# Key transposes in 32x32 blocks on VectorE in place of 128x128 transposes on TensorE, with pooling, softmax and sorted key rows in that layout

## The chip, the cores and the metric

The kernel runs on one core of a Trainium2 chip. The metric is the time of one execution on the device, in microseconds (us). Each run was made on one chip together with runs of the kernel before, so a ratio always compares runs of the same chip. The runs of this study fell on at least four chips, which the results call chips 2, 3, 11 and 13; the number will matter. Every kernel in this document gave correct results, those with useless extra work too.

## The reference, cut to what matters

There are B = 1024 sequences of up to 100 steps with 128 features. A GRU runs over all 100 steps; its hidden states are the keys. A small network scores each key against an item, a masked softmax over the steps gives weights, and the weighted sum of the keys is pooled. The first 100 pooled features, transposed, are the attention weights of a second recurrent loop, the AUGRU, which runs over the same keys. Each sequence takes its AUGRU state at its own last step into a final network.

```python
_, gru_seq = lax.scan(gru_step, h0, swapaxes(item_historical_embedding, 0, 1))
keys = swapaxes(gru_seq, 0, 1)                       # B x 100 x 128
score = _mlp(concat([keys, q, keys - q, q * keys]), att_layers, relu)
attn = softmax(where(mask == 1, score, -inf), axis=1)
pooled = einsum('bt,btd->bd', attn, keys)
att_seq = pooled.T[:T]
def augru_step(h, (x_t, a_t)):
    r = sigmoid(concat([h, x_t]) @ Wr.T + br)
    u = a_t * sigmoid(concat([h, x_t]) @ Wu.T + bu)
    h_hat = tanh(concat([h * r, x_t]) @ Wh.T + bh)
    return (1 - u) * h + u * h_hat
aug_out = scan(augru_step, h0, (keys, att_seq))
attention_feature = aug_out[b, sequential_length[b] - 1]
# ... final three-layer network on user, item, history and attention_feature
```

## The kernel before

Features lie on the 128 partitions and sequences on the columns, in two halves of 512 columns whose steps alternate. In the GRU each half-step's new state is transposed on TensorE, so that pooling can weight a sequence by a scalar of its partition, and so that a sequence's keys can be written to memory as one row. Four steps make a row of 2 KB.

```python
def transpose(self, t):
    q, n = divmod(t, G)                               # G = 4
    ...
    p = pa.tile([P, GH, P], F32, tag="a", name="pk")
    for g in range(GH):                               # 4 groups of 128 sequences
        nc.tensor.transpose(p[:, g, :], h[:, ts(g, P)], ident)
    nc.scalar.copy(kt[:, :, n, :], p)
    if n == G - 1:
        nc.sync.dma_start(out=keys_d[q]..., in_=kt...)
```

The AUGRU runs on sequences sorted by length, longest first, so that the width of a step (the columns still alive) falls from 512 to about 20. The keys come back from memory in sorted order through indirect gathers on GpSimd, 128 rows each, up to four per half and group of four steps. TensorE transposes them again and ScalarE copies them.

```python
def load_rows(q, i, widths):
    ...
    for g in range(-(-widths[q * G] // P)):           # up to 4 gathers
        gather(r[:, g, :], keys_d[q], g, i)           # 128 rows x 2 KB
def load_key(t, i):
    ...
    for g in range(-(-w // P)):
        nc.tensor.transpose(p[:, ts(g, P)], r[:, g, ts(n, P)], ident)
    k = wp.tile([P, HB], F32, name="k3", bufs=6)
    nc.scalar.copy(k[:, :w], p[:, :w])
def step(t, i):                                       # one half-step of the AUGRU, shortened
    pr = gate(wr, h); nc.scalar.activation(pr, pr, Sigmoid); nc.vector.tensor_mul(r, h, pr)
    pu = gate(wu, h); nc.scalar.activation(pu, pu, Sigmoid); nc.vector.tensor_mul(u, pu, at)
    ph = gate(wh, r); nc.scalar.activation(ph, ph, Tanh)
    # VectorE: ph -= h; ph *= u; h += ph
```

The attention weights are sorted between the loops with 32 matmuls against 0/1 matrices that GpSimd builds.

Of the kernel before, what the change touches and what calls it, by code (L numbers as in the profile page):

```python
# [11 lines left out]
I32 = mybir.dt.int32  # L12
AF = mybir.ActivationFunctionType
# [5 lines left out]
P = 128  # L19
# [5 lines left out]
GH = HB // P  # L25
A0, A1 = 80, 40
# [16 lines left out]
NQ = T // G  # L43

AHEAD = 2

# [8 lines left out]
def kernel(ctx: ExitStack, tc: tile.TileContext, a: dict, out: bass.AP):  # L55
# [15 lines left out]

    nc = tc.nc
# [3 lines left out]
    keys_d = [dram.tile([B, G * P], F32, name=f"keys_d{q}") for q in range(NQ)]  # L76
    mask_d = dram.tile([T, B], BF16, name="mask_d")
    inv_d = dram.tile([B, 1], I32, name="inv_d")
    over_d = dram.tile([1, 1], I32, name="over_d")
    att_d = [dram.tile([T, HB], F32, name=f"att_d{i}") for i in range(NH)]  # L80
    rlen_d = dram.tile([NG, P], F32, name="rlen_d")
# [11 lines left out]
    pooled = const.tile([P, NG, P], F32, name="pooled")  # L93
    alive = const.tile([P, NG, T], F32, name="alive")
    idx = const.tile([P, GH, NH], I32, name="idx")
# [4 lines left out]
    def gather(dst, src, g, i):  # L100

        nc.gpsimd.indirect_dma_start(  # L102
            out=dst,
            out_offset=None,
            in_=src,
            in_offset=bass.IndirectOffsetOnAxis(ap=idx[:, g, i : i + 1], axis=0),
        )
# [3 lines left out]
    def load_rows(q, i, widths):  # L111

        r = mid.tile([P, GH, G * P], F32, tag="once", name="rows") if q == 0 else (
            rows["pool"].tile([P, GH, G * P], F32, name="rows")
        )
        for g in range(-(-widths[q * G] // P)):
            gather(r[:, g, :], keys_d[q], g, i)
        rows[q, i] = r

    def gru_phase(pools):  # L120
# [41 lines left out]
        nc.gpsimd.memset(hist, 0.0)  # L162
        q0 = pre.tile([P, B], F32, name="q0")
# [15 lines left out]
        def load_later():  # L179
# [8 lines left out]
            mask_i = mid.tile([P, NG, T], I32, name="mask_i", tag="once")  # L188
            nc.sync.dma_start(
                out=mask_i, in_=a["mask"].rearrange("(g p) t -> p g t", p=P)  # L190
            )
            on = pre.tile([P, NG, T], F32, name="on")
            nc.vector.tensor_scalar(on, mask_i, 1.0, None, ALU.is_equal)
            later["on"] = on
            yield
# [8 lines left out]
            nc.vector.tensor_copy(step, step_i)  # L204
            nc.vector.tensor_tensor(
# [59 lines left out]
            ids = pre.tile([P, NG], I32, name="ids")  # L265
            nc.gpsimd.iota(ids, pattern=[[P, NG]], base=0, channel_multiplier=1)
            own = pre.tile([P, NG], F32, name="own")
            nc.vector.tensor_copy(own, ids)
# [14 lines left out]
            for g in range(NG):  # L283
                nc.gpsimd.indirect_dma_start(
                    out=inv_d,
                    out_offset=bass.IndirectOffsetOnAxis(ap=rank_i[:, g : g + 1], axis=0),
                    in_=ids[:, g : g + 1],
                    in_offset=None,
                )
                yield  # L290

            ranks = pre.tile([P, HB], F32, name="ranks")
            nc.gpsimd.iota(
                ranks,
                pattern=[[NH, HB]],
                base=0,
                channel_multiplier=0,
                allow_small_or_imprecise_dtypes=True,
            )
            later["ranks"] = ranks  # L300
            for i in range(NH):
                r = pre.tile([P, NG], F32, name=f"rank{i}")
                nc.vector.tensor_scalar_add(r, rank, float(-i))
                later[f"rank{i}"] = r
            nc.sync.dma_start(
                out=idx, in_=inv_d.rearrange("(g p i) o -> p g (i o)", p=P, i=NH)
            )
            yield
            for n, shape in (
# [6 lines left out]
                ("user", [P, B]),  # L316
# [10 lines left out]
        class Half:  # L327
            def __init__(self, i):
                self.i = i
                self.cols = ts(i, HB)  # L330
                self.groups = slice(i * GH, (i + 1) * GH)
# [3 lines left out]
                self.s_b = self.top = self.den = None  # L335
# [4 lines left out]
                self.kt = {}  # L340

# [70 lines left out]
            def transpose(self, t):  # L412

                q, n = divmod(t, G)
                h = self.h.pop(t) if t < T - 1 else self.h[t]
                if n == 0:
                    self.kt[q] = kp.tile([P, GH, G, P], F32, name="kt")
                kt = self.kt[q]
                p = pa.tile([P, GH, P], F32, tag="a", name="pk")
                for g in range(GH):  # L420
                    nc.tensor.transpose(p[:, g, :], h[:, ts(g, P)], ident)  # L421
                nc.scalar.copy(kt[:, :, n, :], p)  # L422
                if n == G - 1:
                    nc.sync.dma_start(
                        out=keys_d[q][self.cols, :].rearrange("(g p) f -> p g f", p=P),
                        in_=kt.rearrange("p g n f -> p g (n f)"),
                    )
# [21 lines left out]
            def score(self, t):  # L449
# [5 lines left out]
                if s == b0:  # L455
                    self.s_b = sp.tile([2 * G, HB], F32, name="s_b", bufs=4)
                nc.sync.dma_start(
                    out=self.s_b[s - b0 : s - b0 + 1, :],
                    in_=self.mv[SC[self.i] : SC[self.i] + 1, :],
# [5 lines left out]
            def softmax(self):  # L465
# [5 lines left out]
                on = later["on"][:, self.groups, b0:b1]  # L471
                s_b, top_old, den_old = self.s_b, self.top, self.den
                e = sp.tile([P, GH, 2 * G + 1], F32, name="e", bufs=6)
                top = sp.tile([P, GH], F32, name="top", bufs=5)
                den = sp.tile([P, GH], F32, name="den", bufs=5)
# [3 lines left out]
                def scores():  # L479
                    pt = pa.tile([P, GH, 2 * G], F32, tag="a", name="pt")  # L480
                    for g in range(GH):
                        nc.tensor.transpose(
                            pt[:, g, :n], s_b[:n, ts(g, P)], ident[:n, :n]
                        )
# [4 lines left out]
                    if j:  # L489
# [5 lines left out]
                        top.unsqueeze(2).to_broadcast([P, GH, n]),  # L495
# [3 lines left out]
                def sums():  # L499
                    nc.vector.tensor_mul(e[:, :, :n], e[:, :, :n], on)  # L500
                    nc.vector.tensor_reduce(den, e[:, :, :n], AX.X, ALU.add)
                    if j:
                        old = sp.tile([P, GH], F32, name="old")
# [15 lines left out]
            def pool(self, count, eng):  # L519
                while count and self.todo:  # L520
                    e, n, t = self.todo.pop(0)
                    if t is None:
                        eng.tensor_mul(  # L523
                            pooled[:, self.groups, :],
                            pooled[:, self.groups, :],
                            e[:, :, n].unsqueeze(2).to_broadcast([P, GH, P]),
# [3 lines left out]
                    acc = pooled[:, self.groups, :]  # L530
                    k = self.kt[t // G][:, :, t % G, :]
                    w = e[:, :, n].unsqueeze(2).to_broadcast([P, GH, P])
                    if t == 0:
                        eng.tensor_mul(acc, k, w)
                    else:
                        d = wp.tile([P, GH, P], F32, name="kw")
# [5 lines left out]
            def weights(self):  # L542


                att = hp.tile([P, GH, P], F32, tag="h", name="att")
                nc.vector.memset(att[:, :, T:], 0.0)
                nc.vector.tensor_mul(
                    att[:, :, :T], pooled[:, self.groups, :T], alive[:, self.groups, :]
                )
                nc.vector.tensor_mul(  # L550
                    att[:, :, :T],
                    att[:, :, :T],
                    self.den.unsqueeze(2).to_broadcast([P, GH, T]),
                )
                self.att = att


            def features(self):
# [8 lines left out]
                nc.gpsimd.tensor_mul(cross, item[:, cols], hist[:, cols])  # L567
                part = kp.tile([P, GH, M0], F32, tag="kt", name="part")
                for g in range(GH):
                    b = slice(self.i * HB + g * P, self.i * HB + (g + 1) * P)  # L570
                    comb = (later["user"][:, b], item[:, b], hist[:, b], cross[:, ts(g, P)])
# [14 lines left out]
        def sort_weights():  # L586


            sums = [ps.tile([P, HB], F32, tag="g", name="pw") for _ in range(NH)]
            for g in range(NG):  # L590
                half = halves[g // GH]
                for i, p in enumerate(sums):
                    here = xp.tile([P, HB], F32, tag="x", name="here")
                    nc.gpsimd.tensor_scalar(
                        here,
                        later["ranks"],
                        later[f"rank{i}"][:, g : g + 1],
                        None,
                        ALU.is_equal,
                    )  # L600
                    nc.tensor.matmul(
                        p,
                        lhsT=half.att[:, g % GH, :],
                        rhs=here,
                        start=(g == 0),
                        stop=(g == NG - 1),
                    )
            for i, p in enumerate(sums):
                att = hp.tile([P, HB], F32, tag="h", name="att_t")
                nc.vector.tensor_copy(att, p)  # L610
                first = ps.tile([P, HB], F32, tag="g", name="first")
                nc.tensor.matmul(
                    first,
                    lhsT=ident[:, 0:1].to_broadcast([P, P]),
                    rhs=att,
                    start=True,
                    stop=True,
                )
                nc.scalar.copy(h3[i], first)
                nc.sync.dma_start(out=att_d[i], in_=att[:T, :])  # L620
# [22 lines left out]
        rest = None  # L643

# [54 lines left out]
    def augru_phase(pools, widths):  # L699
# [104 lines left out]
        for i in range(NH):  # L804
            load_key(0, i)
# [99 lines left out]
```

## Time and profile before

| | before |
|---|---|
| time, first three runs | 2379.89 us median (2377.21 to 2382.64) |
| span of the profiled run | 2355.4 us |
| update that writes the last GRU state (hn) starts | 1621.0 us |
| first AUGRU matmul | 1675.7 us |
| TensorE busy, granted clock | 98%, 0.981 |

A page of the profile gives each engine's busy share, then the span in 40 slices with the busy tenths of each engine. The lines quoted in the prediction are read there. One thing in the small table was not read when it should have been: the profiled run took 2357.19 us, and every timed run took 20 to 25 us more. That is 1%, where the three timed runs lie within 0.2% of one another. It comes back below.

### The profile page before, as it was taken

What the parts mean: (1) busy time and instruction counts of PE and PEld (TensorE: products, weight loads), DVE (VectorE), ACT (ScalarE), POOL (GpSimd) and SP (SyncE); (2) the same over time, 40 slices, a digit from 0 to 9 for tenths busy, and PEclk for the clock granted to TensorE, in tenths of its full rate; (3) what the DMA queues carried; (4) which work ended last, traced back from release to release, by engine and by line L of the source; (5) the groups of instructions that cost most, each with busy time, mean ns of one, the idle gap of its engine ahead of it and who ended that gap; (6) DMA issues with size and microseconds to landing.
All of it is one profiled execution on the core that took longest, in us unless ns stands there. A gap on an engine that the chain in (4) does not pass through costs nothing.

```text
span 2355.4 us, 25359 instructions
## 1 busy us (share of the span) xinstructions
PE 2305.8 (98%) x7640; PEld 1194.4 (51%) x7640; DVE 1528.0 (65%) x2733; ACT 1192.8 (51%) x2125; POOL 1165.7 (49%) x1006
## 2 busy tenths in 40 slices
PE   8999999999999999999999999997899999999998
PEld 3444444444444444444444444443445566678987
DVE  7766666666666676766666666665466666666763
ACT  3455545555545555555555554544344444555663
POOL 1356767656566767656565656686512121121210
PEclk9999999999999999999999999998999999999996
DMA  5322232222222221222222222201423332333320
GB/s 155 113 92 93 80 97 97 88 88 88 88 88 83 92 83 56 86 70 88 84 88 87 88 88 88 83 34 71 126 82 95 104 100 70 99 105 81 97 70 7
DMA packets 140854, 204.26 MB, mean 87 GB/s; under 512 B 31023, under 2 KB 77843, under 8 KB 140707
## 3 DMA queue, kind: packets, MB, share of 16 engines
q1 hardware_dynamic: 129410, 167.64, 22.7%
q0 software_dynamic: 11296, 34.92, 5.1%
q8 instruction: 62, 1.02, 0.2%
q14 instruction: 86, 0.70, 0.1%
HBM read 148.20 MB, written 53.87 MB: 86 GB/s over the span
## 4 chain that ended last, share of the span: by engine, by line
PE 88%; POOL 4%; DMA 3%; DVE 2%; ACT 1%; issue 1%; SPq 0%; ACTq 0%; POOLq 0%; DVEq 0%
PE ps L375 38%; PE pm L443 6%; PE pm L444 6%; PE ph L739 4%; PE pr L739 4%; PE pu L737 4%; PE ph L737 4%; PE pu L739 4%; PE pr L737 4%; PE px L630 4%; PE pk L421 3%; PE pk L726 3%; DMA s_b<-mv 2%; POOL pooled L538 1%; POOL kw L537 1%
## 5 line engine op out<-in xcount | busy, mean ns | idle before, releaser
L375 PE MATMUL ps<-hn,whh 128*128 128x512 f32 x1188 | 590.8, 606 | 0.0
L375 PE MATMUL ps<-x,wih 128*128 128x512 f32 x1200 | 582.5, 595 | 4.0 <-DMA x<-in_hist_x 4.0
L375 PEld LDWEIGHTS ps<-hn,whh 128*128 128x128 f32 x1188 | 218.1, 191 | 315.2 <-issue 307.5
L102 POOL DMA_INDIRECT rows<-keys_d,idx x130 | 123.8, 952 | 475.9 <-PE pk L726 435.8
L395 DVE SCALAR_TENSOR_TENSOR u<-ps,bhh,r 128x512 f32<-128x512 f32 x198 | 148.6, 751 | 316.3 <-ACT r L387 255.0
L375 PEld LDWEIGHTS ps<-x,wih 128*128 128x128 f32 x1200 | 213.8, 191 | 198.9 <-issue 191.4
L406 ACT ACTIVATE ps<-ps,bih 128x512 f32<-128x512 f32 x200 | 132.4, 662 | 319.0 <-DVE ps L405 316.8
L363 POOL TENSOR_TENSOR hist<-hist,xm 128x512 f32<-128x512 f32 x200 | 268.6, 1358 | 2.5
L362 POOL TENSOR_TENSOR xm<-x,m 128x512 f32<-128x512 f32 x200 | 244.3, 1239 | 37.1 <-DMA x<-in_hist_x 32.8
L523 POOL TENSOR_TENSOR pooled<-pooled,e 128x512 f32<-128x512 f32 x25 | 26.3, 1052 | 460.1 <-ACT e L497 460.1
L538 POOL TENSOR_TENSOR pooled<-pooled,kw 128x512 f32<-128x512 f32 x190 | 248.1, 1306 | 6.6
L422 ACT COPY kt<-pk 128x512 f32<-128x512 f32 x200 | 117.4, 587 | 246.4 <-PE pk L421 244.8
L408 DVE TENSOR_TENSOR d<-hn,ps 128x512 f32<-128x512 f32 x198 | 136.0, 687 | 136.5 <-ACT ps L406 136.5
L537 POOL TENSOR_TENSOR kw<-kt,e 128x512 f32<-128x512 f32 x190 | 209.5, 1120 | 1.8 <-DVE old L504 0.6
L443 PE MATMUL pm<-hn,wk 128*128 128x512 f32 x400 | 205.9, 596 | 1.8 <-DVE hn L410 1.8
L444 PE MATMUL pm<-kq,wkq 128*128 128x512 f32 x400 | 204.4, 592 | 0.0
L441 DVE TENSOR_TENSOR kq<-hn,item 128x512 f32<-128x512 f32 x200 | 199.4, 997 | 0.9
L447 ACT ACTIVATE mv<-f 128x512 f32<-128x512 f32 x200 | 126.1, 631 | 101.5 <-DMA s_b<-mv 49.5
L639 ACT ACTIVATE mv<-px,bx 41x512 f32<-41x512 f32 x202 | 137.8, 682 | 57.1 <-PE px L630 54.4
L755 DVE TENSOR_TENSOR ph<-ph,h 128x512 f32<-128x512 f32 (+49 forms) x198 | 87.9, 444 | 115.9 <-ACT ph L753 114.9
L421 PEld LDWEIGHTS pk<-ident,hn 128*128 128x128 f32 x800 | 99.9, 141 | 105.5 <-issue 95.6
L405 DVE TENSOR_TENSOR ps<-ps,u 128x512 f32<-128x512 f32 x200 | 140.0, 700 | 20.8 <-DVE u L395 0.5
(139 smaller groups left out, 3552.4 us busy)
## 6 DMA issues: line engine op xcount, KB each, us to landing
x<-in_hist_x SPq DMA_DIRECT2D x212, 256.0 KB, 2.9
keys_d<-kt SPq DMA_DIRECT2D x50, 1024.0 KB, 5.1
m<-mask_d SPq DMA_DIRECT2D x200, 128.0 KB, 3.0
s_b<-mv SPq DMA_DIRECT2D x200, 2.0 KB, 3.1
rows<-keys_d,idx POOLq DMA_INDIRECT x130, 4.2
at<-att_d SPq DMA_DIRECT2D x4, 256.0 KB, 5.7
part_d<-part SPq DMA_DIRECT2D x2, 400.0 KB
item<-in_item SPq DMA_DIRECT2D x1, 512.0 KB
```

What stands on the lines that cost most here:

```text
L362: nc.gpsimd.tensor_mul(d, x, m)
L363: nc.gpsimd.tensor_add(acc, acc, d)
L375: nc.tensor.matmul(p, lhsT=w[:, g, :], rhs=v, start=(j == 0), stop=(j == len(parts) - 1),)
L395: nc.vector.scalar_tensor_tensor(out=u, in0=ph, scalar=bhh[:, 2:3], in1=r, op0=ALU.add, op1=ALU.mult,)
L421: nc.tensor.transpose(p[:, g, :], h[:, ts(g, P)], ident)
L441: nc.vector.tensor_mul(kq, h, item[:, self.cols])
L443: nc.tensor.matmul(p, lhsT=wk[i], rhs=h, start=True, stop=False)
L444: nc.tensor.matmul(p, lhsT=wkq[i], rhs=kq, start=False, stop=True)
L537: eng.tensor_mul(d, k, w)
L538: eng.tensor_add(acc, acc, d)
L737: nc.tensor.matmul(p, lhsT=m[:, 1, :], rhs=k, start=True, stop=v is None)
L739: nc.tensor.matmul(p, lhsT=m[:, 0, :], rhs=v, start=False, stop=True)
```

## The change

The intent is to take transposes off TensorE, which is busy 98% of the span. VectorE transposes the 32x32 blocks of a 128x512 tile in one instruction. After it, a partition holds one sequence of each block of 32 but only 32 of its features, so a sequence's data stand on four partitions, a quarter each. Pooling and softmax work in that layout (scores are broadcast to four rows of a tile `s_b`, and transposed by VectorE too). The key rows in memory become quarter rows: 32 features by eight steps, 1 KB; a gather of 128 quarter rows brings the keys of 32 sequences. VectorE transposes back in the AUGRU. The attention weights are stored and sorted by eight gathers.

```diff
@@ constants
+R = 32
-NQ = T // G
+READ = [G] + [2 * G] * ((T - G) // (2 * G))     # steps per group: 4, 8, 8, ...
+FIRST = [sum(READ[:q]) for q in range(len(READ))]
+GATHER = 70
@@ load_rows
-        for g in range(-(-widths[q * G] // P)):
-            gather(r[:, g, :], keys_d[q], g, i)
+        for k in range(-(-width // R)):              # up to 16 gathers
+            nc.gpsimd.indirect_dma_start(out=r[:, k, :], in_=keys_d[q],
+                in_offset=bass.IndirectOffsetOnAxis(ap=idx_k[:, k, i : i + 1], axis=0), ...)
+            yield
@@ transpose (GRU)
-                for g in range(GH):
-                    nc.tensor.transpose(p[:, g, :], h[:, ts(g, P)], ident)
-                nc.scalar.copy(kt[:, :, n, :], p)
+                nc.vector.transpose(kt[:, :, n, :], h.rearrange("p (k r) -> p k r", r=R))
@@ score
+                    out=s_b.rearrange("(p r) f -> p r f", r=R)[:, s - b0, :],
+                    in_=self.mv[...].unsqueeze(1).to_broadcast([1, P // R, HB]),
@@ load_key (AUGRU)
-            for g in range(-(-w // P)):
-                nc.tensor.transpose(p[:, ts(g, P)], r[:, g, ts(n, P)], ident)
-            nc.scalar.copy(k[:, :w], p[:, :w])
+            nc.vector.transpose(k[:, :w, :], rows[q, i][:, :w, ts(t - FIRST[q], R)])
@@ AUGRU loop
+        load_group(1)                                # 32 gathers, both halves
         for t in range(T):
-                if n == 0 and 0 < q < NQ - 1:
-                    load_rows(q + 1, i, widths)
+            if t in FIRST[1:-1]:
+                load_group(FIRST.index(t) + 1)       # up to 32 gathers at once
... (index arithmetic for quarter rows, pooling and softmax by R, weights by gathers)
```

## The prediction

> **What bounds the kernel now.** I read the page first (busy shares, slices, chain), then the timeline of one stretch of the GRU and one of the AUGRU, then the groups. From the page:
>
> ```profile
> PE 2305.8 (98%) x7640; PEld 1194.4 (51%) x7640; DVE 1528.0 (65%) x2733; ACT 1192.8 (51%) x2125; POOL 1165.7 (49%) x1006
> ...
> PE   8999999999999999999999999997899999999998
> ...
> DVE  7766666666666676766666666665466666666763
> ...
> POOL 1356767656566767656565656686512121121210
> ...
> PE 88%; POOL 4%; DMA 3%; DVE 2%; ACT 1%; issue 1%; SPq 0%; ACTq 0%; POOLq 0%; DVEq 0%
> PE ps L375 38%; PE pm L443 6%; PE pm L444 6%; PE ph L739 4%; PE pr L739 4%; PE pu L737 4%; PE ph L737 4%; PE pu L739 4%; PE pr L737 4%; PE px L630 4%; PE pk L421 3%; PE pk L726 3%; DMA s_b<-mv 2%; POOL pooled L538 1%; POOL kw L537 1%
> ```
>
> TensorE is busy 98% and is nine tenths in nearly every slice, and the chain that ended last lies on it for 88%. VectorE stands at six to seven tenths, GpSimd at five to seven until the GRU ends near 1,617 us, and at one to two after. So time taken off TensorE comes off the end, if VectorE, which gets the work, keeps up. The timeline of the GRU, where a half-step is one step of one of the two halves of 512 sequences:
>
> ```profile
> 822.65 0.60 PE L421 MATMUL pk<-ident,hn 128*128 128x128 f32 x4
> ...
> 823.09 1.02 PE L375 MATMUL ps<-x,wih 128*128 128x512 f32 x2
> ...
> 825.73 0.68 DVE L441 TENSOR_TENSOR kq<-hn,item 128x512 f32<-128x512 f32 x1
> ...
> 828.51 0.75 DVE L395 SCALAR_TENSOR_TENSOR u<-ps,bhh,r 128x512 f32<-128x512 f32 x1 [2.09 <-ACT r L387]
> ...
> 829.36 0.70 DVE L405 TENSOR_TENSOR ps<-ps,u 128x512 f32<-128x512 f32 x1
> ...
> 830.10 0.66 ACT L406 ACTIVATE ps<-ps,bih 128x512 f32<-128x512 f32 x1 [1.62 <-DVE ps L405]
> ...
> 830.79 0.69 DVE L408 TENSOR_TENSOR d<-hn,ps 128x512 f32<-128x512 f32 x1 [0.73 <-ACT ps L406]
> ```
>
> The four key transposes start at 822.65 and the next matmul at 823.09: 0.44 us of TensorE per half-step, 0.11 each (their 0.60 is overlap). On VectorE the last operation of a half-step (kq) starts at 825.73 and the next half-step's first (u) waits until 828.51; it has some 2 us to spare there, and 0.7 us more while ScalarE computes the tanh (830.10 to 830.79). The AUGRU:
>
> ```profile
> 1723.98 0.60 PE L726 MATMUL pk<-ident,rows 128*128 128x128 f32 x4
> ...
> 1724.42 1.00 PE L737 MATMUL pr<-k,wr 128*128 128x498 f32 x2
> ...
> 1737.01 0.95 POOL L102 DMA_INDIRECT rows<-keys_d,idx  x1 [0.30 <-issue]
> ...
> 1738.26 0.95 POOL L102 DMA_INDIRECT rows<-keys_d,idx  x1 [0.31 <-issue]
> ```
>
> Again 0.44 us of transposes per half-step while four groups of 128 sequences live (fewer later). The last two rows show gathers issued 1.25 us apart.
>
> ```profile
> L441 DVE TENSOR_TENSOR kq<-hn,item 128x512 f32<-128x512 f32 x200 | 199.4, 997 | 0.9
> ...
> L102 POOL DMA_INDIRECT rows<-keys_d,idx x130 | 123.8, 952 | 475.9 <-PE pk L726 435.8 <-issue 30.9 <-PE pr L739 7.5
> ...
> L728 ACT COPY k<-pk 128x512 f32<-128x512 f32 (+48 forms) x200 | 77.1, 387 | 6.8 <-PE pk L726 4.0 <-DMA att_d<-att_t 1.3 <-PE ph L737 0.7
> ...
> L505 DVE TENSOR_TENSOR den<-den,old 128x4 f32<-128x4 f32 x28 | 23.3, 835 | 0.8
> ```
>
> [...] The kernel before has no VectorE transpose, so no row shows it[...]. [...] kq, which reads two SBUF tiles, averages 0.997 us where an undisturbed one takes 0.68, and a 128x4 sum takes 0.835. [...] The key rows are now written in pieces of exactly 512 B (16x128 elements per partition) instead of 2 KB.
>
> **The change, part by part.**
>
> GRU, TensorE. Gone are 200 groups of four key transposes: 200 x 0.44 = 88 us. The 30 score transposes held it 0.34 us each in the chain: 10 us. Together 98 us of about 1,590, some 15.9 us per step going to 14.9.
>
> GRU, VectorE. Before, from u to the end of kq takes 6.06, 5.69 and 5.72 us in three half-steps of that stretch (802.83, 811.55 and 820.67 on), tanh wait included. One transpose adds 0.6 to 0.7: about 6.5. A half-step of TensorE becomes 7.45. Once in 6.7 half-steps a softmax block adds a 0.69 us score transpose and seven operations over 128 columns in place of 32, some 0.1 us longer each: in all about 4 us per block against 3 before, an average of 0.6. VectorE then needs about 7.1 of 7.45. It fits, with little left. The built order puts the score transpose into the tanh wait, which helps. I charge 5 us for jitter: GRU -93.
>
> GRU, ScalarE and GpSimd. ScalarE loses 200 copies of 0.59 us, off the path. GpSimd keeps its pooling, same counts and elements, at about 10 of now 14.9 us per step, and takes 32 gathers of first keys (8 before). The built order puts them in bursts of 7, 9 and 11 in the first tenth of the GRU, 11 x 1.25 = 14 us at worst. Inputs are two steps ahead, so I charge 5 us, small index loads included.
>
> Between the loops. Before, 32 matmuls sort the weights in 17 us from 1,653.65, and the AUGRU's first matmul starts at 1,675.7. The last weights are ready near 1,657. After: a store of them (4 us, from issue-to-landing medians of 3 to 5), four gathers (5 us) with 3 us landing, transposes, copy, matmul and copy (3 us): near 1,672, so -4.
>
> AUGRU, TensorE. 512 transposes x 0.11 = 56 us, and 200 ScalarE copies off the path. While more than 256 sequences live (about 52 steps) TensorE paces the step: a step took 10.36 us at step 10 and 7.06 at step 40. That part holds 52 steps x 2 halves x 3 to 4 transposes, about 40 us, and I count all of it. Later VectorE, with 12 in place of 10 operations per step, is level with TensorE (at 180 columns 12 x 0.34 = 4.1 us against a measured 4.5 less 0.44), and in the last 20 steps the period of 3.2 us is the recurrence itself. There I count 3 us. So -43.
>
> AUGRU, start. Rows are now gathered per 32 sequences: the next eight steps' keys need 16 gathers per half, 32 x 1.25 = 40 us of GpSimd, begun only behind the weight gathers, near 1,668. The built order places the two transposes that wait for them inside AUGRU step 1. The second can run near 1,668 + 40 + 4 = 1,712, where an unhindered loop, starting at 1,672, would be there at about 1,685. [...] everything stops: +27. Later groups have eight steps of at least 3 us for ever fewer gathers and stay hidden.
>
> Sum: -93 + 5 - 4 - 43 + 27 = -108; 2,380 - 108 = 2,272 us.
>
> **The rivals.**
>
> A: VectorE becomes the bound of the GRU, because the fp32 transpose takes twice the estimate (1.3 us) or is held up by GpSimd. For it: 7.1 of 7.45 us is already counted[...]. [...] A half-step near 7.75 us would leave 40 us of the GRU's gain and make late AUGRU steps longer: about 2,330.
>
> B: the first gathers do not stall the AUGRU, as GpSimd starts sooner or the row pitch is shorter. Against: 1.25 us is steady in the trace. Then 2,245.
>
> C: GpSimd's pooling slows in the new layout (runs of 32 in place of 128), or the 512 B key rows delay the score rows and input loads behind them. For it: ScalarE already waits 49.5 us on score-row transfers. Against: GpSimd has a third of the step free and DMA engines are busy two to three tenths. A fifth more pooling time costs nothing; half again with delays, 2,300 to 2,340.
>
> D: all of the TensorE time comes out, 98 + 56 + 17, and nothing is given back: 2,209.
>
> **Range and chances.** The terms are uncertain by about 30 (VectorE in the GRU), 20 (AUGRU start), 15 (late steps) and 15 (GpSimd and DMA): together some 43, so 2,215 to 2,335 around 2,272. The 2% line is at 2,332; only A or C at their worst reach it. Faster 0.88, within 2% 0.09, slower 0.03.
>
> **What would show it.** Right: VectorE transposes of 0.69 to 0.75 us, GRU steps of 14.9 to 15.1 us with TensorE still nine tenths busy, VectorE near 75% over the span; a hole of some 27 us on all compute engines in AUGRU step 1, ended by a gather; full-width AUGRU steps 0.88 us shorter, the last 20 unchanged at 3.2. Wrong: TensorE waiting for hn in every GRU step (A), no hole at the start (B), inputs or score rows late (C). My weakest figures are the transpose's duration, which no trace here shows, and the hole.

## The result, and the profile after

The changed kernel took **2467.51 us** (2458.93 to 2471.84, four runs) against 2378.64 us (2377.21 to 2382.64, four runs) on the same chip: a ratio of 1.0366, 95% interval 1.0335 to 1.0398, **slower by 3.7%**. The prediction said faster, and its range ended at 2335. A ratio here is the mean time of one kernel's fast runs over that of the other's in the same rounds, so it is not quite the ratio of the medians.

The page of the kernel after: busy times, then the rows of TensorE, VectorE, ScalarE, GpSimd and of TensorE's clock in 40 slices of 61.75 us, then the chain of waits by engine.

```profile
PE 2211.2 (90%) x6184; PEld 1093.0 (44%) x6184; DVE 1723.1 (70%) x3175; ACT 995.7 (40%) x1729; POOL 1276.1 (52%) x1121
...
PE   8998899999999999999999998544987898888898
...
DVE  7798667777878777777777787722755666666652
ACT  3343344444444444444444444311332333344432
POOL 0169977666666666666666669364213303222200
PEclk9999999999999999999999999866988988999875
...
PE 24%; another core or an unknown queue 3%; issue 3%; DVE 2%; ACT 1%; DMA 0%; POOL 0%; DVEq 0%; POOLq 0%
```

TensorE lost 95 us of work, as intended. For the first 25 slices, most of the GRU, its row looks nearly as before. The next three, from 1,544 us, read 5, 4 and 4, and VectorE, ScalarE and the clock fall with it; then it stands at 7 to 9 where before had nines. In the last two of those three slices GpSimd stands at 6 and 4, which is one burst of gathers. The chain breaks off after 24% of the span, "at another core or an unknown queue".

Groups of the kernel after by line (busy us, mean ns, then idle time just before and what ended it), first VectorE's:

```profile
L482 DVE STREAM_TRANSPOSE kt<-hn 128x512 f32<-128x512 f32 x200 | 140.0, 700 | 0.0
...
L772 DVE STREAM_TRANSPOSE k<-rows 128x512 f32<-128x512 f32 (+15 forms) x200 | 92.9, 466 | 81.5 <-PE ph L784 30.5 <-DMA rows<-keys_d,idx_k 24.1 <-remote 15.2
```

The gathers, among GpSimd's groups:

```profile
L130 POOL DMA_INDIRECT rows<-keys_d,idx_k x250 | 240.3, 961 | 480.6 <-DVE k L772 375.9 <-issue 71.7 <-DVE ph L803 26.7
```

And two of ScalarE's groups:

```profile
L510 ACT ACTIVATE mv<-f 128x512 f32<-128x512 f32 x200 | 125.9, 630 | 468.9 <-DVE f L509 304.6 <-DMA s_b<-mv 150.8 <-issue 13.4
L800 ACT ACTIVATE ph<-ph,bh 128x512 f32<-128x512 f32 (+48 forms) x200 | 91.9, 459 | 204.4 <-PE ph L786 137.4 <-remote 45.2 <-issue 9.1
```

The transposes cost what was expected: 0.70 us each in the GRU. The expectation was the author's own estimate: the trace of before has no VectorE transpose, and its other 128x512 operations on VectorE took 0.68 to 0.75 us on average, but for kq with 0.997. GpSimd issues 250 gathers in place of 130. ScalarE waits 150.8 us (49.5 before) for the score rows to leave the tile `mv`, and its tanh in the AUGRU waits 45.2 us for something "remote", which no group showed before.

By time: the update of the last hn starts at 1566.6 us (before: 1621.0) and the AUGRU starts at 1623.4 (1675.7). So this trace is 52 us ahead there. From its first matmul to the end of the span the AUGRU then takes 846.6 us, in the trace of before 679.7: all of the loss, and more, is there. The timeline of ScalarE alone, during the first burst of 62 gathers (both halves of the second and of the third group without a pause, 1622.7 to 1703 us with two gathers of the final network behind them):

```profile
1668.41 0.66 ACT L796 ACTIVATE pu<-pu,bu 128x512 f32<-128x512 f32 x1 [11.93 <-remote]
1678.91 0.66 ACT L800 ACTIVATE ph<-ph,bh 128x512 f32<-128x512 f32 x1 [9.84 <-remote]
1689.41 0.66 ACT L793 ACTIVATE pr<-pr,br 128x512 f32<-128x512 f32 x1 [9.84 <-remote]
1700.61 0.66 ACT L796 ACTIVATE pu<-pu,bu 128x512 f32<-128x512 f32 x1 [10.54 <-remote]
```

The start, the length, the operation and in brackets the idle time before it and what ended it. ScalarE executes one instruction in 10 us. The matmul whose result the tanh at 1678.91 reads had ended at 1668.7, ten us earlier, and VectorE and TensorE follow as soon as ScalarE delivers (VectorE 0.03 us after the end of the one at 1689.41, TensorE 0.06 us after VectorE). No instruction of ScalarE waits for a gather; in the built order its only waits are on TensorE and VectorE. The same picture stands in the second half of the later bursts (28, 24 and ever fewer gathers), once every eight steps: from 1860 to 1900 us, with the 24, TensorE is busy 26.75 us of 40, from 1900 to 1945, without gathers, 43.28 of 45.

### The profile page after: what moved, and what is told of

Read it like the earlier page. It is cut to its first block, busy times and chain, and to the rows that moved or that the text cites. A ratio compares the mean times of both kernels' runs of the same rounds, so it can differ in the third digit from the quotient of the medians.

```text
span 2470.0 us, 22200 instructions
## 1 busy us (share of the span) xinstructions
PE 2211.2 (90%) x6184; PEld 1093.0 (44%) x6184; DVE 1723.1 (70%) x3175; ACT 995.7 (40%) x1729; POOL 1276.1 (52%) x1121
## 5 line engine op out<-in xcount | busy, mean ns | idle before, releaser
L438 PE MATMUL ps<-x,wih 128*128 128x512 f32 x1200 | 597.1, 607 | 20.2 <-ACT r L450 10.4
L438 PE MATMUL ps<-hn,whh 128*128 128x512 f32 x1188 | 576.0, 594 | 0.4 <-DVE hn L473 0.4
L130 POOL DMA_INDIRECT rows<-keys_d,idx_k x250 | 240.3, 961 | 480.6 <-DVE k L772 375.9
L786 PE MATMUL ph<-r,wh 128*128 128x512 f32 (+55 forms) x396 | 150.3, 465 | 148.5 <-DVE r L794 92.0
L599 POOL TENSOR_TENSOR pooled<-pooled,kw 128x512 f32<-128x512 f32 x190 | 258.4, 1360 | 6.7
L426 POOL TENSOR_TENSOR hist<-hist,xm 128x512 f32<-128x512 f32 x200 | 258.7, 1308 | 2.4
L800 ACT ACTIVATE ph<-ph,bh 128x512 f32<-128x512 f32 (+48 forms) x200 | 91.9, 459 | 204.4 <-PE ph L786 137.4
L793 ACT ACTIVATE pr<-pr,br 128x512 f32<-128x512 f32 (+49 forms) x198 | 90.5, 457 | 181.9 <-PE pr L786 107.0
L786 PEld LDWEIGHTS ph<-r,wh 128*128 128x128 f32 x396 | 74.9, 217 | 194.9 <-DVE r L794 118.2
L796 ACT ACTIVATE pu<-pu,bu 128x512 f32<-128x512 f32 (+48 forms) x200 | 91.6, 458 | 154.6 <-PE pu L786 70.4
```

The source lines that it names most:

```text
L130: nc.gpsimd.indirect_dma_start(out=r[:, k, :], out_offset=None, in_=keys_d[q], in_offset=bass.IndirectOffsetOnAxis(ap=idx_k[:, k, i : i + ...
L426: nc.gpsimd.tensor_add(acc, acc, d)
L438: nc.tensor.matmul(p, lhsT=w[:, g, :], rhs=v, start=(j == 0), stop=(j == len(parts) - 1),)
L599: eng.tensor_add(acc, acc, d)
L786: nc.tensor.matmul(p, lhsT=m[:, 0, :], rhs=v, start=False, stop=True)
```

## The experiments

Theories. **T1**: long unbroken runs of indirect gathers on GpSimd hold ScalarE up. **T2**: it is the bytes, or the number of row pieces, not their grouping. **T3**: ScalarE now issues transfers itself (stores of the weights), and that slows it. **T4**: VectorE's transposes in the AUGRU's order, or late keys, are the cause. **T5**: part of the GRU's missing gain comes from the gathers and 512-byte rows there, which delay the score rows and the input loads. Labels that begin with a are made from the kernel after, those with b from before. Bare times are medians; "held" and "quiet" chips are explained with the runs that told them apart.

| run | chip | this, us | before there, us | ratio (95%) |
|---|---|---|---|---|
| a_spread3 | 13 | 2350.91 | 2375.81 | 0.9896 (0.9882–0.991) |
| b_burst28 | 13 | 2700.6 | 2375.81 | 1.1364 (1.1348–1.138) |
| b_burst7 | 13 | 2595.19 | 2375.81 | 1.093 (1.0911–1.0948) |
| a_early | 13 | 2440.49 | 2375.81 | 1.0272 (1.0254–1.029) |
| b_plain28 | 13 | 2393.99, one run | 2375.04 | |
| b_work28 | 13 | 2406.66, one run | 2375.04 | |
| b_narrow28 | 13 | 2708.7, one run | 2375.04 | |
| a_best | 13 | 2309.27 | 2375.04 | 0.9725 (0.9705–0.9745) |
| b_burst7b | 11 | 2356.17, one run | 2353.85 | |
| b_pace28 | 11 | 2471.68, one run | 2353.85 | |
| a_early_sb | 11 | 2278.26 | 2353.85 | 0.968 (0.9664–0.9696) |
| a_best2 | 11 | 2265.92 | 2353.85 | 0.9618 (0.959–0.9646) |
| after_r | 2 | 2468.47 | 2378.41 | 1.0376 (1.0351–1.0402) |
| b_burst28_r | 2 | 2713.56, one run | 2378.41 | |
| a_early_sb_r | 2 | 2442.68 | 2378.41 | 1.0264 (1.0235–1.0292) |
| a_best2_r | 2 | 2280.42 | 2378.41 | 0.9585 (0.9551–0.9619) |
| after_r2 | 3 | 2302.41 | 2354.91 | 0.9778 (0.9762–0.9794) |
| before_r | 3 | 2351.89, one run | 2354.91 | |

Where there is a ratio, all runs were of the fast state. One-run results have no state and are used only where the effect is large.

### Spread the gathers of the AUGRU

GpSimd copies one column of the half-step's `u` into the gather's target first, so the gather cannot be issued earlier; three are dealt out per half-step.

```diff
         for k in range(-(-width // R)):
+            if gate_on:
+                nc.gpsimd.tensor_copy(r[:, k, 0:1], gate_on[0][:, 0:1])   # u of this half-step
             nc.gpsimd.indirect_dma_start(
@@ AUGRU loop
-                load_group(FIRST.index(t) + 1)
+                todo += [load_rows(q, i, widths[FIRST[q]], kp) for i in range(NH)]
 ...
                 step(t, i)
+                for _ in range(3):
+                    while todo and next(todo[0], True):
+                        todo.pop(0)
```

> The kernel after, with the key gathers of groups 2 and later issued three at a time after each half-step of the AUGRU (each held back by a copy of one column of that half-step's u) in place of bursts of 24 to 32; the first burst of 62 loses only its second half. T1 (long bursts of GpSimd gathers hold up ScalarE): the AUGRU falls from about 830 us to 650 to 690, the whole to 2300 to 2350 us. T2 (the bytes or the number of row pieces are the cause, not their grouping) and T4 (the VectorE transposes in the AUGRU's order are the cause): no change, 2440 to 2480 us.

2350.91 us: 117 us less than the kernel after, just past the end of T1's range. From its first matmul to the end of the span the AUGRU takes 730.6 us (after: 846.6), where T1 had asked for 650 to 690. Bytes, row pieces and VectorE's transposes are unchanged, so T2 and T4 fall for most of the loss. The first burst of 62 was left as it was, and at narrow widths three gathers per half-step are again an almost unbroken run.

### Put a burst into the kernel before

GpSimd has little to do in the AUGRU of before (131.42 us of the 680 from 1675 on). Nine bursts of 28 useless gathers were added, one every eight steps.

```diff
+        def extra(n):
+            nc.gpsimd.tensor_copy(spare[:, :, 0], us[0][:, :32])          # holds the burst to this step
+            for j in range(n):
+                gather(spare[:, j, :], part_d, j % GH, 0)                 # 128 rows x 800 bytes
 ...
+            if t % 8 == 2 and 10 < t < 90:
+                extra(28)
```

> The kernel before, with nine bursts of 28 useless gathers (128 rows of 800 bytes) added to GpSimd in the AUGRU, one every 8 steps. GpSimd is otherwise nearly idle there. T1: each burst holds ScalarE up for 10 to 20 us, the whole goes from 2379 to 2470 to 2560 us, and ScalarE's instructions stand about 10 us apart in the second half of each burst. T2, T4: within 1%, 2375 to 2400 us.

2700.6 us: the loss is 325 us, 36 us for each burst of 35 us, more than T1 asked. Most of the bursts follow gathers of the kernel's own without a pause, so that the unbroken runs are 28 to 38 long. ScalarE in the first of them (the added 28 go from 1876 to 1911 us, the run begins at 1866):

```profile
1891.33 0.59 ACT L754 ACTIVATE ph<-ph,bh 128x426 f32<-128x426 f32 x1 [6.41 <-issue]
1900.48 0.51 ACT L728 COPY k<-pk 128x420 f32<-128x420 f32 x1 [8.56 <-remote]
1910.93 0.59 ACT L746 ACTIVATE pr<-pr,br 128x426 f32<-128x426 f32 x1 [9.94 <-remote]
```

The same rows as in the kernel after, in a kernel that has no VectorE transpose and lets ScalarE issue nothing: T3 and T4 are out as causes of the hold. The hold builds up: the idle times before ScalarE's instructions are 2.96, 3.64, 6.41, 8.56 and 9.94 us, one after the other. DMA engines were busy 0.38 of the time from 1876 to 1911 us and 0.32 from 1890 on, where TensorE did nothing; in b_plain28 below they are busy 0.71 from 2305.5 to 2313.5 us, and ScalarE is not held. So it isn't their load.

> The kernel before, with about as many useless gathers (273) as in the run with bursts of 28, but in bursts of 7 every second step. T1: no hold-up, within 1% of 2379 us. T2 (number and bytes of gathers): as slow as the run with bursts of 28.

2595.19 us: neither theory's number. The windows of this run explain it (from and to, length, then busy us and instructions of TensorE, its weight loads, VectorE, ScalarE and GpSimd; clock, DMA share, GB/s):

```profile
1806.00:1816.00 10.00, 10.00 (x33) 5.21 (x32) 6.07 (x11) 4.66 (x8) 6.88 (x8) 1.00 0.39 109
1826.00:1836.00 10.00, 10.00 (x33) 5.35 (x32) 6.16 (x11) 4.59 (x8) 6.90 (x9) 1.00 0.36 106
1838.00:1848.00 10.00, 6.78 (x16) 3.40 (x15) 2.21 (x4) 1.13 (x2) 5.87 (x7) 0.75 0.75 228
1852.00:1862.00 10.00, 9.93 (x33) 5.46 (x33) 6.04 (x11) 4.45 (x8) 6.88 (x8) 1.00 0.43 109
```

A burst of seven alone (the first and the last row) stops nothing. The one at 1827 runs into the kernel's own eight gathers, 15 in a row from 1827.2 to 1845.7; some nine gathers in, from 1838 on, ScalarE does 1.13 us in 10. Every second added burst met the kernel's own so: the 220 us are 11 on average for each of these 20. T1's premise, a run of up to seven is harmless, held; my choice of steps let the runs join.

### What about the burst is it?

Three variants of the run with 28, each with one line of the burst changed (b_narrow28 also fills a small table, `thin_d`, beforehand):

```diff
-                gather(spare[:, j, :], part_d, j % GH, 0)
+b_plain28:     nc.gpsimd.dma_start(out=spare[:, j, :], in_=part_d[ts(j % NG, P), :])
+b_work28:      nc.gpsimd.memset(spare.rearrange('p a b -> p (a b)')[:, ts(j % 5, 1280)], 0.0)
+b_narrow28:    gather(spare[:, j, 0:1], thin_d, j % GH, 0)                # rows of 4 bytes
```

> As the run of before with bursts of 28, but the 28 useless transfers are plain ones (128 rows of 800 bytes, one after the other in memory, no index), issued by GpSimd. If it is the issuing of many transfers by GpSimd back to back that holds ScalarE up: about 2600 to 2700 us, as with gathers. If it is the indirect form: about 2380 to 2400 us.

> The same bursts with 28 fills of 128x1280 elements on GpSimd, about 1.2 us each, in place of the gathers. If a busy GpSimd by itself [...] holds ScalarE up: 2600 us or more. T1, which puts it down to the transfers it issues: 2375 to 2395 us.

> The same bursts of 28 gathers, with rows of 4 bytes in place of 800. T1 (count and pace of the gathers): about 2650 to 2700 us, as with 800 bytes. T2 (bytes moved): 2380 to 2420 us.

Plain transfers from GpSimd: 2394 us, 19 over before. 28 of them take GpSimd 15 us. Fills: 2407 us, 32 over, a little more than asked. Gathers of 4-byte rows: 2709 us, as long as with 800 bytes. So it is the indirect form in a long run, and neither the bytes (T2 falls), nor the number of transfers, nor a busy GpSimd. Whether the count or the pace of the run decides, these three don't tell; a_best below does in part. By which path inside the chip a gather reaches ScalarE, no run tells.

### The first group's gathers, in the GRU

In after they are meant for step 70 on, but nothing holds them there, and in the built order they stand in runs of 7, 9 and 11 at 222 to 269 us.

```diff
                 if s >= GATHER:
+                    gate_on[:] = [half.prev]      # the hidden state of the step before
                     next(early[half.i], None)
```

> The kernel after, with the gathers of the first key group held back by a copy of one column of a hidden state, so that they stand one per half-step from step 70 of the GRU, not in bursts of 7 to 11 at 195 to 270 us. If those bursts took the 20 us that the GRU lost between 100 and 300 us: 2440 to 2455 us. If the loss there came from the GRU's own start (mask loads, scatters, mask broadcasts): unchanged within 0.3%, 2460 to 2475 us.

2440.49 us, 27 less than after, inside the first theory's range. The window from 200 to 300 us in after:

```profile
200.00:300.00 100.00, 83.78 (x191) 32.71 (x190) 73.89 (x97) 36.28 (x57) 91.06 (x82) 0.95 0.33 98
```

The same window in this run:

```profile
200.00:300.00 100.00, 95.26 (x231) 38.81 (x230) 71.02 (x109) 41.79 (x65) 79.41 (x65) 0.99 0.30 92
```

TensorE is idle 16 us of 100 with the bursts and 5 us without. The last hn comes at 1550.6 us, 16 earlier than in after. Only these 16 us are the edit's: the rest of the 27 lies in the AUGRU, which the edit leaves alone and whose time on held chips varies (827.4 us here, 846.6 in after, 842.8 in after_r). That the sum fell inside the range is partly luck.

### All of it together

```diff
-READ = [G] + [2 * G] * ((T - G) // (2 * G))
+READ = [G, G] + [2 * G] * ((T - 3 * G) // (2 * G)) + [G]   # a short second group
-        early = [load_rows(0, i, HB, mid) for i in range(NH)]      # one gather per half-step
+        early = [chain(*(load_rows(q, i, HB, mid) for q in range(2 - i))) for i in range(NH)]
-GATHER = 70
+GATHER = 45
+                pace = -(-NH * -(-widths[FIRST[q]] // R) // 12)   # gathers per half-step
-        xp = pools.enter_context(tc.tile_pool(name="xp", bufs=8))    # space for it
+        xp = pools.enter_context(tc.tile_pool(name="xp", bufs=7))
... (the gating of the two kernels above; one e buffer less; the rows of keys_d to match READ)
```

> The kernel after with everything T1 asks for: the first key group's gathers held to one per half-step of the GRU; the second group cut to 4 steps, one half of it gathered in the GRU too; all later groups spread over 12 half-steps, as many per half-step as their width needs (3, later 2 and 1). T1: 2265 to 2300 us, that is 27 us off for the GRU's part, some 23 for the start of the AUGRU and some 30 for the remaining holds, from 2351 us of the run with three per half-step. If the holds of that run have another cause: 2315 to 2330 us.

2309.27 us, **2.7% faster than before**, and 9 us outside the range I gave T1. Nearly all of the 9 is in the GRU, which lost 8 us of what a_early had won (last hn at 1558.7); one x buffer less and more gathers there came together, and no run parts them. Its trace also answers a question that the bursts left open: from 1796 to 1833 us, on a held chip, it issues 26 gathers in threes, one three every 4.3 to 4.4 us, 1.44 us apart on average, and ScalarE has no idle time over 1.5 us there. So there a short pause after every three was enough, and the count alone doesn't make a hold. (Closer together, 14 at 1.34 us on average from 2085 us in a_spread3, one idle time of 3.4 us is seen.) In a next version (a_best2 below) the gathers are dealt in fractions and the store of the scores moves to ScalarE's queue. Its call also had two controls, and the queue alone on top of a_early:

### Bursts meant to stand apart, gathers slowed down, and the score rows on another queue

For the two controls on before, bursts of 7 every fourth step, and bursts of 28 slowed down:

```diff
+b_burst7b:   if t % 4 == 2 and 10 < t < 90: extra(7)
+b_pace28:    if j > 1: nc.gpsimd.tensor_copy(spare[:, j, 0:1], spare[:, j - 2, 0:1])   # before each gather
```

> The kernel before with bursts of 7 useless gathers of 800-byte rows again, but only every 4 steps, midway between the kernel's own bursts of 6 to 8, so that they do not run into one another (133 to 140 extra gathers). In the run with 7 every second step, those bursts that followed the kernel's own without a pause held ScalarE up, and those alone did not. If the length of an unbroken run of gathers decides: 2378 to 2400 us. If their number does: about half of that run's loss of 220 us, near 2485 us.

2356.17 us, no loss. But the trace shows that the bursts did not stay apart: most run into the kernel's own, in runs of 9 to 19 gathers. By T1 some of them should have held ScalarE up.

> The kernel before with nine bursts of 28 useless gathers, but each gather held back until the one two before it has landed (a small copy on GpSimd reads its result), so about 1.7 to 2 us apart in place of 1.25. If the pace decides [...]: no hold, 2380 to 2410 us. If an unbroken run of more than some 10 to 16 is enough at any pace: over 2550 us.

2471.68 us, 118 us over before: neither number. No hold is in its trace; TensorE is busy 239.95 us of the 240 from 1820 to 2060. Later GpSimd has more than fits into the eight steps, and VectorE waits for it to release `u` (59.8 us in five waits): a fault of my experiment. Both these runs turned out worthless for T1, as the ones after them show.

The score rows on ScalarE's queue, beside the gated first group of a_early:

```diff
-                nc.sync.dma_start(
+                nc.scalar.dma_start(
                     out=s_b.rearrange("(p r) f -> p r f", r=R)[:, s - b0, :],
```

> The kernel after with the first group's gathers held to one per half-step (2440 us), and the score rows sent to the broadcast tile s_b by ScalarE's queue in place of SyncE's. T5: part of the GRU's missing gain is ScalarE waiting for mv until SyncE's queue has sent older rows to s_b (150.8 us of such waits in after, 49.5 before); then 2422 to 2434 us. If those waits are slack, or the issuing costs ScalarE as much: 2436 to 2460 us.

2278.26 us: **162 us less** than a_early, where T5 asked for some ten. Only part of it is the GRU: its last hn is at 1537.3 us, 13 earlier than in a_early, as the waits of ScalarE for the s_b transfer are gone at the GRU's end (there one of 13.5 us stood). (The two runs are of different chips; the repetition on chip 2 below ends its GRU at 1536.7.) The other 146 us are the AUGRU: the burst of 62 is there unchanged, and ScalarE is not held up in it at all.

```diff
-                pace = -(-NH * -(-widths[FIRST[q]] // R) // 12)
+                pace = NH * -(-widths[FIRST[q]] // R) / 13
-                for _ in range(pace):
+                due += pace if todo else -due
+                while due >= 1:
+                    due -= 1
... (and s_b sent by nc.scalar)
```

> As the best so far (2309 us), with the later groups' gathers dealt evenly over 13 half-steps (2.5 per half-step falling to 0.6, no whole numbers rounded up) and s_b sent by ScalarE's queue. T1: the AUGRU's remaining stalls between 1880 and 2220 us (about 25 us of idle TensorE) shrink: 2280 to 2300 us. If they are not holds by gathers: 2300 to 2315 us.

2265.92 us, 14 better than asked, but this run says nothing of T1, as will be seen. All four runs of this call were on chip 11, where before takes 2354 us in place of 2376. So two things had changed, the queue of s_b and the chip.

### The chip or the queue?

> The kernel after, unchanged, again. If the hold is a matter of the chip and this is a chip where before takes about 2354 us: 2285 to 2320 us, no hold of ScalarE in the bursts. If this is a chip where before takes about 2376 us, or the hold is the kernel's own on any chip: 2440 to 2475 us.

> The kernel before with nine bursts of 28 useless gathers, again. Hold a matter of the chip, and a chip without it: 2355 to 2385 us. Hold on any chip: 2660 to 2705 us.

> The kernel after with the first group's gathers held to one per half-step and s_b sent by ScalarE's queue, again. If the queue of s_b took the hold away: about 2280 to 2300 us on any chip. If the chip did: 2280 us on a chip where before takes 2354 us, and 2420 to 2435 us where it takes 2376 us.

> The best version (spread, fewer at once, s_b on ScalarE's queue), again: 2260 to 2270 us on a chip where before takes 2354 us; where it takes 2376 us, 2280 to 2300 us if T1 holds and pacing is the cure there.

The call fell on chip 2, where before takes 2378 us. The kernel of 2278 us, unchanged, took **2442.68 us** there, with the hold back; after took 2468 and the burst kernel 2714 us. (The first and the last of these lie 8 and 9 us above their ranges.) So it was not the queue: **the hold is on chips 2 and 13 and not on chip 11.** A chip with the hold is called held here, one without it quiet. The best version took 2280 us, ratio 0.9585; its AUGRU takes 691.8 us where that of a_early_sb_r takes 846.3, and 679.3 on chip 11: some 12 us of hold are left in its first steps, where its gathers still stand in a run.

> The kernel after, unchanged, for a chip of the other kind. Where before takes about 2354 us: 2285 to 2315 us (2278 us of the kernel with two parts mended, plus 13 us for s_b and up to 20 us for the first group's gathers), no hold. Where it takes about 2376 us: 2460 to 2475 us, nothing new from this run.

> The kernel before, unchanged, profiled. Where it takes about 2376 us: the 20 us that it is slower than its profile at hand show as ScalarE waiting in the AUGRU near its own gathers, where two of its bursts of 8 meet; if they are spread over the whole run instead (a slower chip throughout), the hold has no part in them. Where it takes about 2354 us: no difference from the profile at hand.

This call fell on chip 3, where before takes 2355 us, and the unchanged kernel after took **2302.41 us, 2.2% faster than before**. It is the same program that is 3.7% slower on the other kind. ScalarE on this chip, in the same burst of 62:

```profile
1671.74 0.66 ACT L796 ACTIVATE pu<-pu,bu 128x512 f32<-128x512 f32 x1 [1.05 <-PE pu L786]
1673.45 0.66 ACT L800 ACTIVATE ph<-ph,bh 128x512 f32<-128x512 f32 x1 [1.05 <-PE ph L786]
1675.16 0.66 ACT L793 ACTIVATE pr<-pr,br 128x508 f32<-128x508 f32 x1 [1.04 <-PE pr L786]
1676.86 0.66 ACT L796 ACTIVATE pu<-pu,bu 128x508 f32<-128x508 f32 x1 [1.04 <-PE pu L786]
```

One instruction every 1.71 us, while gathers go on every 1.26 us. The time of a half-step of the AUGRU, mean over four steps, from the starts of the updates of h, shows where the held chip loses:

| from step | width | before, chip 3 | after, chip 3 | after, chip 2 |
|---|---|---|---|---|
| 1 | 512 | 5.53 | 7.04 | 11.71 |
| 5 | 498 | 5.33 | 4.90 | 4.89 |
| 9 | 476 | 5.13 | 4.69 | 7.51 |
| 13 | 456 | 4.92 | 4.48 | 4.48 |
| 17 | 436 | 4.72 | 4.28 | 6.50 |
| 21 | 416 | 4.52 | 4.08 | 4.07 |
| 41 | 312 | 3.38 | 3.04 | 4.50 |
| 57 | 230 | 2.56 | 2.30 | 3.56 |
| 85 | 88 | 1.63 | 2.10 | 2.67 |
| 89 | 66 | 1.59 | 2.88 | 2.88 |

Between bursts the two chips agree to a hundredth of a microsecond. The last column jumps every eight steps, where a burst stands. What makes a chip held is not known. Chip 13 was held in two calls, and each other chip had one, so something else that changed between the calls isn't ruled out.

Does before itself suffer on a held chip? It was never profiled on one. But six of the b kernels were profiled on held chips, and their extra work begins only after step 10. From AUGRU step 1 to step 4 they need more than before on chip 3 (33.3 us): b_burst28, b_work28, b_plain28 and b_burst7 11.6 to 12.5 us, b_burst28_r 9.5 and b_narrow28 7.1; from there to step 10 they need no more. In that stretch before issues 18 gathers in a row. ScalarE in b_plain28:

```profile
1689.20 0.66 ACT L746 ACTIVATE pr<-pr,br 128x512 f32<-128x512 f32 x1 [3.63 <-PE ph L737]
1695.49 0.66 ACT L749 ACTIVATE pu<-pu,bu 128x512 f32<-128x512 f32 x1 [5.62 <-remote]
1699.75 0.66 ACT L754 ACTIVATE ph<-ph,bh 128x512 f32<-128x512 f32 x1 [3.60 <-remote]
```

So some 7 to 12 of before's 22 us between the two kinds of chips are, by this inference, one hold of its own. The rest is not in the GRU (last hn at 1618.2 us in b_burst28 on chip 13 and in before on chip 3) and not before step 10; after that every one of these kernels has extra work, and no run tells.

## Why the prediction was wrong, point by point

Even on a quiet chip the gain is 53 us, half of the 108 forecast. There the sum can be checked term by term (after on chip 3 against before on chip 3):

| term | predicted | measured | from |
|---|---|---|---|
| GRU with bursts of early gathers | -93 + 5 | -54 | last hn 1564.5 against 1618.2 us |
| between the loops | -4 | +3 | 57.0 against 54.1 us |
| AUGRU start | +27 | +23 | 79.4 against 56.1 us to step 5 |
| AUGRU TensorE | -43 | -40 | steps 5 to 85: 508.9 against 549.3 us |
| last 15 steps | inside the -43 | +15 | step 85 to the last update: 71.6 against 56.8 us |
| sum | -108 | -53 | measured 2302.41 - 2354.91 = -52.5 |
| hold of ScalarE, held chips only | none | +166 | AUGRU 842.8 (chip 2) against 676.5 us |

**The step that failed** is the sentence "Later groups have eight steps of at least 3 us for ever fewer gathers and stay hidden". As far as keys being late goes it was right: after the start VectorE never waits for rows. But it treated a burst on an engine off the path as free, and on the chip of the result each burst stopped ScalarE. With that one term, -53 + 166 gives +113, where the runs on chip 2 show 90; the rest is that before, too, is 23.5 us slower there (2378.41 against 2354.91), which isn't in that sum. The figure could not have been read from the trace of before: its bursts of 8 stand alone but for the 18 at the start, and the trace at hand shows no hold even there. By its time, 2357 us against 2377 to 2383 in the timed runs, it came from a chip of the quiet kind; that is inferred from the time, as the chip of that run isn't recorded. The difference of 1% was in front of me and asked for a reason.

**The GRU was mis-sized by 34 us**, all of it before step 28. From step 28 to 92 a step takes 15.05 us in place of 15.97, 59 us less in all, and the sum asked for 0.93 less per step: that rate was right. But the first 28 steps take 472.6 us against 461.5, 11 more where some 26 less were due. The largest part are the early bursts, which I charged 5 us: held to one per half-step (a_early against after, both on held chips), step 28 comes 22 us sooner, and the last hn 16. They block GpSimd 9 to 14 us each (and stand at 222 to 269 us, past the first tenth of the GRU), and what GpSimd owes is late: on chip 3 SyncE's queue waits 40 us of the 70 from 215 to 285 us for GpSimd to have read older inputs, the score rows stand in that queue behind the input loads, and VectorE waits 10.58 us for them. The rest, some 15 us, no run isolates; from 100 to 170 us VectorE is busy 68.57 of 70 us (44.81 in before), with the transposes and the sorting of the lengths at once, and TensorE does 65.02 us where it did 70.00. The 13 us of a_early_sb are hardly a part of the miss: ScalarE's wait for the score rows at the GRU's end is 13.57 us in after and was 11.35 in before (both on chip 3), so that this gain was open to both kernels. I had a sum of 49.5 us of such waits in hand and let it pass as harmless; it became 150.8.

**The AUGRU's start was right** on a quiet chip; on a held one the first burst adds 37 of the 166 us to it (116.8 us to step 5 in after_r, 79.4 in after_r2). The hole came where the order said, ended by a gather, in two waits of VectorE, which started nothing else in them (10.57 and 13.26 us, here on chip 3):

```profile
1642.52 0.71 DVE L772 STREAM_TRANSPOSE k<-rows 128x512 f32<-128x512 f32 x1 [10.57 <-DMA rows<-keys_d,idx_k]
...
1662.68 0.71 DVE L772 STREAM_TRANSPOSE k<-rows 128x512 f32<-128x512 f32 x1 [13.26 <-DMA rows<-keys_d,idx_k]
```

**The last steps were wrong in sign.** I had them unchanged. Windows of after on chip 3; the number to read is the clock, behind GpSimd's column:

```profile
2216.00:2224.00 8.00, 6.71 (x49) 6.10 (x50) 4.26 (x25) 3.26 (x12) 0.00 (x0) 0.92 0.07 17
2224.00:2232.00 8.00, 7.69 (x35) 7.33 (x35) 2.22 (x13) 2.60 (x9) 0.00 (x0) 0.50 0.04 10
```

The windows of before on chip 3 around its own fall of the clock:

```profile
2294.00:2302.00 8.00, 7.96 (x66) 7.50 (x67) 4.90 (x27) 4.55 (x20) 0.00 (x0) 1.00 0.09 17
2302.00:2310.00 8.00, 7.67 (x47) 7.55 (x47) 3.54 (x19) 3.31 (x15) 0.00 (x0) 0.65 0.06 9
```

The granted clock drops to 0.50 for good near step 88 in after and near step 93 in before. In the trace of after on the chip of the result, pairs of matmuls 72 to 82 columns wide start 0.22 us apart near 2381 us, at a clock of 1.00, and 0.42 us apart near 2388 us, at 0.50. In the 8 us just ahead of the fall TensorE is busy 6.48 us in after and 7.63 in before (both on chip 3), and the drop comes some five steps earlier with the transposes gone. No run varied that alone, so it is not shown that the transposes kept the clock up. Having them on TensorE doesn't by itself keep it up: in b_plain28 they are there, added transfers leave TensorE busy 6.60 us of 8, and the clock falls near step 88 too. Its last 15 steps take 70.8 us against 56.8 in before on chip 3.

**The rivals.** A: not as put, 0.70 us; but for 70 us at the start of the GRU VectorE was full. B: no, the hole came. C: in part, score rows and inputs did come late, but around the early bursts (16 us); at the GRU's end the rows cost no more than before. D: no. None of them was the one that came. (The prediction's four uncertainties give 42 us in squares, not 43, which changes nothing.)

**Right in mechanism**: the duration of the transposes, the step of the GRU and VectorE's room in it from step 28 on, the half-step of the AUGRU shorter by 0.44 us at full width (5.33 to 4.90), the hole.

## What to carry to other kernels

A burst on an engine off the path wasn't free here: the AUGRU of the same program took 842.8 us on chip 2, where GpSimd's runs of gathers held ScalarE up, and 676.5 us on chip 3. Before multiplying the number of indirect gathers, count how many would stand in a row without a pause, and tie them to the steps of the loop, a few at a time, by a small dependency; the version that does so (a_best2) is the fastest on both kinds of chips, some 4% below before. When the profiled run and the timed runs of the same kernel differ by 1%, find out why before predicting 5%, and repeat a surprising result on another chip before explaining it.

## What the runs showed of the chip

- A run of indirect gathers on GpSimd held ScalarE up on some chips and not on others. On chips 2 and 13: from some ten gathers 1.25 us apart on, ScalarE's idle times grow from 3 to 10 us until the run ends (2.96 to 9.94 us in b_burst28); seven or eight in a row are harmless (b_burst7), and so are 26 with a pause after every third (1.44 us apart on average, a_best); 28 plain DMAs or 28 fills of 128x1280 elements don't hold it (19 and 32 us lost over nine bursts); rows of 4 bytes hold as rows of 800 do (2708.7 us against 2700.6).
- Chips differ in this: the same program took 2468.47 us on chip 2 and 2302.41 us on chip 3.
- A VectorE fp32 transpose of a 128x512 tile took 0.70 us in the GRU, 0.70 to 0.71 us in the AUGRU.
- An indirect gather of 128 rows on GpSimd was 0.95 to 0.96 us busy, and in a run the next one started 1.25 to 1.26 us after it, for rows of 800 bytes (b_plain28), 1 KB (after) and 2 KB (before); 28 plain transfers took GpSimd 15 us in b_plain28.
